# Moving an output eviction forward among a step's convolution taps, and sending a layer norm's variance through PSUM

## The chip, the core and the metric

The kernel runs on one core of a Trainium2 chip. The metric is device time in microseconds. Three runs of the kernel before took 3875.0, 3877.8 and 3879.05 us; the median is 3877.8 us.

## The reference

Two layers are computed on a tensor x of 2 images, 768 channels and 64 × 64 pixels, all in float32. Each is `x = x + layer(group_norm(x))`. The first layer is a Mamba-like block with 1536 inner channels, and the change touches only this one. The second is an attention over tokens with a softmax over heads; it matters here as the work that follows.

```python
x = hs @ in_proj_w.T                                  # 768 -> 1536
xs = depthwise_conv3x3(x) + conv_b                    # 9 taps per channel
xs = xs * sigmoid(xs)
dt, Bs, Cs = split(xs_seq @ x_proj_w.T)
delta = softplus(dt @ dt_w + dt_b)
dA  = exp(delta * A);  dBu = delta * u * Bs           # 4 states per channel
states = scan over tokens: s = dA * s + dBu
y = sum_n(states * Cs) + D_param * u
y = (y - mean(y)) * rsqrt(var(y) + 1e-05) * ln_g + ln_b   # layer norm over the 1536 channels
out = y @ out_proj_w.T                                # 1536 -> 768
```

## The kernel before

The first layer is cut into 16 tiles of 512 tokens (8 image rows), and each tile into 12 chunks of 128 channels. One call of `step(g)` handles one chunk of the scan, and 192 chunks in all (`g` from 0 to 191; tile `g // 12`, chunk `g mod 12`). The same step works on other chunks too: the convolution runs 15 chunks ahead (`a = g + AHEAD`), the input projection 17 ahead (`n`), and the output projection one tile behind (`BEHIND = 12`). The steps run under a manual schedule: each engine executes its instructions in exactly the order in which the Python code issues them, and semaphores hold only what really depends. An engine's queue is strictly in order, so an instruction that waits holds up everything behind it.

What one step issues, engine by engine, as far as it matters here:

- **TensorE (PE):** the input projection (L336), the sums for the layer norm (L518, odd steps), the output projection into the two-bank PSUM tile `po` (L551), in one step of each tile the averages `pm` for the layer norm (L529), and up to one convolution tap as a product with a diagonal matrix (L401), for the next step's chunk.
- **VectorE (DVE):** the convolution taps that are left to it (`taps_dve`, L415: four or five; the first ones accumulate in the PSUM tile `acc`, the last one writes the SBUF tile `u`), then in every fourth step the output's eviction (`out_evict`, L563: two multiplications of `po` by the reciprocal deviation `rs`, into SBUF slots), then the three long instructions of the scan: the input product (L489), the scan itself (L491) and the product with C (L498). In steps with `g mod 12 = 3` it adds the two instructions of the variance (`norm_rs2`, L535 and L536) at the end.
- **ScalarE (ACT):** SiLU (L420, a group of four each fourth step), softplus (L461), the middle tap into `acc` (`tap_act`, L374, which has to wait for the last DVE tap of the chunk before, since `acc` is a single buffer), the input projection's eviction (L349), scaled copies for the taps that a DMA adds (L386), the exponentials of the scan (L466), the output's sums (L585), and the layer norm's square (L531), logarithm (L537) and exponential (L538), the last of which writes `rs`.
- **GpSimd (POOL):** the sum over states (`sum1`, L478), delta times u (`du`, L470, which the input product of the scan in the same step reads), and the issue of accumulating DMAs: convolution taps (L392, L395), the terms of y (L485) and the residual (`out_residual`, L571).
- **SyncE (SP):** plain DMAs: weights, inputs, the store of the result.

`out_evict(g)` evicts what the output projection of the four steps before has accumulated. There is a single `po`, so the first product of the output projection in the same step (L551) waits until both evictions have read it. It happens at `g mod 12` = 4, 8 and 0, three times for each tile. The reciprocal deviation `rs` of a tile is computed at the end of the step with `g mod 12 = 3`; the eviction at `g mod 12 = 4` is the first that uses it. Both `po` evictions have `rs` as their SBUF input and `po` as their PSUM input.

In the steps with an eviction the convolution chunk has `a mod 4 = 3`, and DVE has four taps (3, 5, 7 and 8), three into `acc` and the last into `u`. From `g = 177` on there are no more taps; in those steps the eviction is the first thing that DVE does.

Around the change, in `step`:

```python
if 0 <= a < NQ0:
    taps_dve(a)
if BEHIND < g <= NQ0 + BEHIND and (g - BEHIND) % 4 == 0:
    out_evict(g)
...
if do_c:
    out_proj(g)
if rs_now:
    norm_rs2(g // KI - 1, *norm_rs(g // KI - 1))
if 0 <= a + 1 < NQ0:
    taps_pe(a + 1)
```

Of the kernel before, what the change touches and what calls it, by code (L numbers as in the profile page):

```python
# [9 lines left out]
ALU = mybir.AluOpType  # L10
# [24 lines left out]
NQ0 = NI * KI  # L35
# [17 lines left out]
BEHIND = 12  # L53
# [13 lines left out]
def both_layers(  # L67
# [45 lines left out]
    def take():  # L113
        return slots.pop(0)
# [244 lines left out]
    def dma_taps(a):  # L359
        return DMA_TAPS[a % 4] if a >= AHEAD else ()  # L360

    def pe_taps(a):
        return PE_TAPS[a % 4] if a >= AHEAD else FILL_TAPS
# [39 lines left out]
                skip_group_check=True,  # L403
            )

    def taps_dve(a):
        c = a % KI
        taps = [j for j in range(9) if j != 4 and j not in pe_taps(a) + dma_taps(a)]
        xs, acc = xs_bufs[a % 2], accs.pop(a).rearrange("p (h w) -> p h w", w=W)
        u = take()  # L410
        us[a] = u
        for j in taps:
            dy, dx = divmod(j, 3)
            dst = u.rearrange("p (h w) -> p h w", w=W) if j == taps[-1] else acc
            nc.vector.scalar_tensor_tensor(  # L415
                dst, xs[:, dy : dy + TR, dx : dx + W], pc[:, c, PC_W + j : PC_W + j + 1], acc, ALU.mult, ALU.add
            )

    def silu(a):
        nc.scalar.activation(us[a], us[a], AF.Silu, bias=pc[:, a % KI, PC_CB : PC_CB + 1])  # L420
# [15 lines left out]
    def x_sum(i):  # L436
        px = psX.tile([P, 512], F32, tag="px", name=f"pxs{i}")
        nc.tensor.matmul(px[:XM, :], xsum, pxs["halves"], start=True, stop=True)
        give(pxs.pop("halves"))
        pxs["sum"] = px  # L440
# [91 lines left out]
        return pm, mu2  # L532

    def norm_rs2(i, pm, mu2):
        nc.vector.scalar_tensor_tensor(mu2, mu2, -1.0, pm[:, 1, :], ALU.mult, ALU.add)  # L535
        nc.vector.tensor_scalar_max(mu2, mu2, 0.0)  # L536
        nc.scalar.activation(rs, mu2, AF.Ln, bias=eps_c)  # L537
        nc.scalar.activation(rs, rs, AF.Exp, scale=-0.5)  # L538

# [17 lines left out]
    def out_evict(g):  # L557

        po = pos[0]
        i, r = (g - 1 - BEHIND) // KI, (g - 1) % KI  # L560
        for e in range(2):
            xr = take()
            nc.vector.tensor_mul(xr, po[:, e, :], rs)  # L563
            xrs[i, 2 * (r // 4) + e] = xr
# [311 lines left out]
    with tc.manual_schedule():  # L876
# [17 lines left out]
        def step(g, prep=None):  # L894
            a, n = g + AHEAD, g + AHEAD + 2
# [27 lines left out]
                norms[g][0][1]()  # L923
            if xd_now:
                x_sum(g // KI + 1)
            if 0 <= a < NQ0:
                taps_dve(a)
            if BEHIND < g <= NQ0 + BEHIND and (g - BEHIND) % 4 == 0:
                out_evict(g)
            for q in range((v - 1) * PER_STEP, min(v * PER_STEP, N_PIECE)):  # L930
                if q >= 0:
                    gn_piece(1, q)
# [96 lines left out]
            if rs_now:  # L1029
                norm_rs2(g // KI - 1, *norm_rs(g // KI - 1))  # L1030
# [16 lines left out]
        with tc.tile_pool(name="l0st", bufs=1, side="right") as sp:  # L1047
            wg = out_weights_load(sp)
            for g in range(-AHEAD - 2, -1):
                step(g, (lambda: out_weights(sp, wg)) if g == -AHEAD + 5 else None)  # L1050
                if g >= -AHEAD + 7:
                    for k in ((g + AHEAD - 7) * 2, (g + AHEAD - 7) * 2 + 1):
                        if k < KI:
                            out_weights_store(wg, k)
# [10 lines left out]
        for g in range(-1, NQ0 + 2):  # L1065
            step(g)
# [18 lines left out]
        for g in range(NQ0 + 2, NQ0 + BEHIND + 3):  # L1085
            step(g)
# [12 lines left out]
@with_exitstack  # L1099
def mamba_then_attention(  # L1100
    ctx, tc, x, in_wP, xp_wP, dt_wP, out_wT, pc_in, comb_in, pick_in, xsum_in, qkvP, woutP, temp_c, ident_in, gavg_in, gsel_in, hcol_in, hsel_in, esel_in, out
):
    nc = tc.nc
    keep = ctx.enter_context(tc.tile_pool(name="keep", bufs=1))
    dram = ctx.enter_context(tc.tile_pool(name="dram", bufs=1, space=DRAM))
    x1 = [dram.tile([DM, L], F32, name=f"x1_{b}") for b in range(NB)]

    stats1 = [keep.tile([P, KM, 2 * NT + 1], F32, name=f"stats1_{b}") for b in range(NB)]

    ident = keep.tile([P, P], F32, name="ident")  # L1110
    nc.sync.dma_start(ident, ident_in)
    ones = keep.tile([P, P], F32, name="ones")
    nc.vector.memset(ones, 1.0)
    eps_c = keep.tile([P, 1], F32, name="eps_c")
    nc.vector.memset(eps_c, EPS)
    consts = (ident, ones, eps_c)


    wo_dr = dram.tile([KM // 2, KI // 3, P, 3, 2 * P], F32, name="wo_dr")
    bc_dr = [dram.tile([2 * NS, TL], F32, name=f"bc_dr{i}") for i in range(NI)]  # L1120
    both_layers(
        tc, nc, consts, x, in_wP, xp_wP, dt_wP, out_wT, pc_in, comb_in, pick_in, xsum_in, gavg_in, gsel_in, wo_dr, bc_dr, x1, stats1,
        qkvP, woutP, temp_c, hcol_in, hsel_in, esel_in, [out[b].rearrange("c h w -> c (h w)") for b in range(NB)],
    )
# [104 lines left out]
```

## Time and profile before

| what | value |
|---|---|
| median of three runs | 3877.8 us |
| the profiled execution's own time | 3880.97 us |
| its span | 3879.2 us |
| mean granted TensorE clock | 0.985 |
| busy PE / DVE / ACT / POOL | 3643.6 / 2792.9 / 2459.8 / 1657.2 us |
| evictions L563: count, median | 96, 682 ns |
| variance L535 and clamp L536: count, median | 16 each, 680 ns and 1731 ns |
| taps L415 into `acc`: count, mean | 753, 754 ns |
| taps L415 into `u`: count, mean | 192, 748 ns |

The span is that of one execution under the profiler; the device time lies 1.8 us above it. A row of the profile's groups names the line, the engine, the operation, the output and inputs by the program's names, and the shapes; then busy time and mean duration; then the idle time of the engine just ahead of these instructions, and what ended it. The first layer's steps with scans and taps fill the span from about 380 to 2580 us; the scans without taps end near 2800 us, and the attention layer fills the rest.

### The profile page before, as it was taken

How to read it: one execution, taken by the hardware profiler on the slowest of the kernel's cores; microseconds unless marked ns; L12 is line 12 of the kernel's file. 1: busy time of each engine (PE TensorE's matmuls, PEld its weight loads, DVE VectorE, ACT ScalarE, POOL GpSimd, SP SyncE). 2: the span in 40 equal slices, each digit the busy share in tenths (PEclk: the TensorE clock that was granted, in tenths of full speed). 3: DMA queues.
4: the chain of work that ended last, by engine and by line, in shares of the span. 5: the costliest groups of instructions: out<-in, count | busy, mean ns of one | idle time of the engine just before them, and what ended most of it. 6: DMA issues, size and time to landing. Idle time of an engine off the chain costs nothing.

```text
span 3879.2 us, 32882 instructions
## 1 busy us (share of the span) xinstructions
PE 3643.6 (94%) x9798; PEld 1512.8 (39%) x9798; DVE 2792.9 (72%) x2339; ACT 2459.8 (63%) x4667; POOL 1657.2 (43%) x1494
## 2 busy tenths in 40 slices
PE   4977999999999999999999999999999999998999
PEld 2422333333333333333433333333344444444444
DVE  5699999999999999999999999987400520005311
ACT  1378888888898888888888888886423511123000
POOL 0435556555655655655555655554300011111222
PEclk9988999999999999999999999999999999999999
DMA  7466898888888889889888898886543245442454
GB/s 278 160 177 134 187 205 180 201 202 194 203 182 200 205 188 207 179 202 213 172 203 183 202 206 184 198 176 168 146 126 129 68 145 154 150 140 83 142 179 154
DMA packets 321574, 679.65 MB, mean 175 GB/s; under 512 B 37378, under 2 KB 45572, under 8 KB 317300
## 3 DMA queue, kind: packets, MB, share of 16 engines
q0 software_dynamic: 139248, 253.56, 38.2%
q1 hardware_dynamic: 182148, 424.00, 33.4%
q8 instruction: 78, 1.28, 0.1%
q14 instruction: 100, 0.82, 0.1%
HBM read 393.77 MB, written 55.31 MB: 116 GB/s over the span
## 4 chain that ended last, share of the span: by engine, by line
DVE 45%; PE 34%; ACT 7%; issue 6%; DMA 5%; POOL 3%; SPq 0%; DVEq 0%; POOLq 0%; ACTq 0%
DVE s L491 17%; PE mm L665 13%; DVE acc L415 9%; PE mm L638 9%; DVE da L498 8%; DVE s L489 7%; PE pa L336 3%; PE po L551 3%; DMA tm<-tm 2%; PE pq L638 2%; DMA u<-tm 2%; POOL ysum L478 1%; DMA u<-ysum 1%; DVE u L563 1%; ACT da L466 1%
## 5 line engine op out<-in xcount | busy, mean ns | idle before, releaser
L551 PE MATMUL po<-u,w 128*128 128x512 f32 x2304 | 1047.8, 605 | 69.1 <-DVE u L563 68.7
L336 PE MATMUL pa<-u,w 128*128 128x512 f32 (+1 forms) x2304 | 1040.0, 601 | 0.0
L491 DVE TENSOR_TENSOR_SCAN s<-da,s 128x2052 f32<-128x2052 f32 x192 | 851.1, 4433 | 19.2 <-DVE s L489 0.5
L551 PEld LDWEIGHTS po<-u,w 128*128 128x128 f32 x2304 | 431.5, 192 | 673.8 <-issue 569.1
L336 PEld LDWEIGHTS pa<-u,w 128*128 128x128 f32 x2304 | 430.4, 192 | 591.4 <-issue 529.0
L478 POOL TENSOR_TENSOR ysum<-da 128x1024 f32<-128x1024 f32 x192 | 396.7, 2066 | 533.1 <-DVE da L498 506.9
L415 DVE SCALAR_TENSOR_TENSOR acc<-xs,pc,acc 128x512 f32<-128x512 f32 x753 | 567.8, 754 | 70.3 <-PE acc L401 50.3
L466 ACT ACTIVATE da<-dl,neg_a 128x512 f32<-128x512 f32 x768 | 489.6, 713 | 0.0
L660 POOL TENSOR_TENSOR w<-w,at 128x768 f32<-128x768 f32 x96 | 141.0, 1470 | 814.9 <-DMA w<-woutP 562.5
L392 POOL DMA_DIRECT2D tm<-tm x310 | 273.9, 885 | 500.5 <-ACT tm L386 444.9
L489 DVE TENSOR_TENSOR s<-du,bc 128x2048 f32<-128x2048 f32 x192 | 438.8, 2285 | 66.0 <-POOL du L470 63.8
L498 DVE TENSOR_TENSOR da<-s,bc 128x2048 f32<-128x2048 f32 x192 | 440.0, 2292 | 6.3
L485 POOL DMA_DIRECT2D u<-ysum x384 | 391.7, 1314 | 0.5 <-POOL ysum L478 0.3
L665 PE MATMUL mm<-u,w 128*128 128x512 f32 x684 | 320.8, 596 | 0.0
L386 ACT ACTIVATE tm<-xs,pc 128x512 f32<-128x512 f32 x487 | 317.7, 718 | 2.8 <-DMA tm<-tm 2.8
L674 DVE TENSOR_TENSOR u<-mm,u 128x512 f32<-128x512 f32 x59 | 40.8, 692 | 337.8 <-PE mm L665 337.8
L374 ACT ACTIVATE acc<-xs,pc 128x512 f32<-128x512 f32 x192 | 132.6, 690 | 211.7 <-DVE u L415 210.8
L470 POOL TENSOR_TENSOR du<-dl,u 128x512 f32<-128x512 f32 x192 | 258.7, 1348 | 0.0
L395 POOL DMA_DIRECT2D u<-tm x177 | 218.7, 1235 | 83.5 <-DMA tm<-tm 64.5
L665 PE MATMUL mm<-v,w 128*128 128x512 f32 x468 | 225.7, 593 | 0.0
L638 PE MATMUL mm<-u,w 128*128 128x512 f32 x456 | 214.4, 594 | 0.0
L665 PEld LDWEIGHTS mm<-u,w 128*128 128x128 f32 x684 | 129.3, 191 | 167.6 <-issue 167.4
(206 smaller groups left out, 4060.1 us busy)
## 6 DMA issues: line engine op xcount, KB each, us to landing
u<-ysum POOLq DMA_DIRECT2D x384, 256.0 KB, 5.8
tm<-tm POOLq DMA_DIRECT2D x310, 256.0 KB, 4.7
w<-in_wP SPq DMA_DIRECT2D x192, 384.0 KB, 4.3
w<-wo_dr SPq DMA_DIRECT2D x192, 384.0 KB, 5.1
u<-x SPq DMA_DIRECT2D x254, 256.0 KB, 4.3
u<-tm POOLq DMA_DIRECT2D x177, 256.0 KB, 5.8
w<-qkvP SPq DMA_DIRECT2D x96, 384.0 KB, 3.1
w<-woutP SPq DMA_DIRECT2D x96, 384.0 KB, 3.7
```

The lines of the kernel that those rows point to most:

```text
L336: nc.tensor.matmul(pa[:, :nn], w[:, k, :], xts[i, k][:, :nn], start=(k == 0), stop=(k == KM - 1))
L386: nc.scalar.activation(tm.rearrange("p (h w) -> p h w", w=W), xs[:, dy : dy + TR, dx : dx + W], AF.Copy, scale=pc[:, c, PC_W + j : PC_W + ...
L415: nc.vector.scalar_tensor_tensor(dst, xs[:, dy : dy + TR, dx : dx + W], pc[:, c, PC_W + j : PC_W + j + 1], acc, ALU.mult, ALU.add)
L466: nc.scalar.activation(das[g % 2][:, n, 1:], deltas[g], AF.Exp, scale=neg_a[:, c, n : n + 1])
L478: nc.gpsimd.tensor_add(ysum[:, 0 : 2 + g % 2 : 1 + g % 2, :], da[:, 0:2, 1:], da[:, 2:4, 1:])
L485: nc.gpsimd.dma_start(us[g], ysums(g, n), accum_op=ALU.add)
L489: nc.vector.tensor_mul(s[:, :, 1:], dus.pop(g).unsqueeze(1).to_broadcast([P, NS, TL]), bc[:, :NS, :])
L491: nc.vector.tensor_tensor_scan(sf, das[g % 2].rearrange("p n l -> p (n l)"), sf, 0.0, ALU.mult, ALU.add)
L498: nc.vector.tensor_mul(das[g % 2][:, :, 1:], s[:, :, 1:], bc[:, NS:, :])
L551: nc.tensor.matmul(po[:, e, :], w[:, kk, e * P : (e + 1) * P], us[i * KI + k], start=(k == 0), stop=(k == KI - 1))
L638: nc.tensor.matmul(pa, w[:, k, :], x1s[b, j, k], start=(k == 0), stop=(k == KM - 1))
L665: nc.tensor.matmul(po, w[:, k, :], w1s[b, k, j], start=(k == 0), stop=(k == KM - 1))
```

## The change

There are two edits. `taps_dve` takes a function and calls it after it has issued the first tap; `step` passes it the eviction in the steps that have one. So on DVE the two evictions stand behind the first tap and ahead of the other three. In steps without taps the eviction is issued where it was. `norm_rs2` writes the difference of mean square and squared mean to the first half of the PSUM tile `pm`, whose contents have been read by then, and the clamp at zero reads it there and writes the SBUF tile `mu2` as before.

```diff
-    def taps_dve(a):
+    def taps_dve(a, after_first):
...
             nc.vector.scalar_tensor_tensor(
                 dst, xs[:, dy : dy + TR, dx : dx + W], pc[:, c, PC_W + j : PC_W + j + 1], acc, ALU.mult, ALU.add
             )
+            if j == taps[0]:
+                after_first()
...
     def norm_rs2(i, pm, mu2):
-        nc.vector.scalar_tensor_tensor(mu2, mu2, -1.0, pm[:, 1, :], ALU.mult, ALU.add)
-        nc.vector.tensor_scalar_max(mu2, mu2, 0.0)
+        nc.vector.scalar_tensor_tensor(pm[:, 0, :], mu2, -1.0, pm[:, 1, :], ALU.mult, ALU.add)
+        nc.vector.tensor_scalar_max(mu2, pm[:, 0, :], 0.0)
...
+            evict = (lambda: out_evict(g)) if BEHIND < g <= NQ0 + BEHIND and (g - BEHIND) % 4 == 0 else (lambda: None)
             if 0 <= a < NQ0:
-                taps_dve(a)
-            if BEHIND < g <= NQ0 + BEHIND and (g - BEHIND) % 4 == 0:
-                out_evict(g)
+                taps_dve(a, evict)
+            else:
+                evict()
```

## Prediction

> **What bounds the kernel now.** I read the page first: engine shares, chain that ended last, costliest groups.
>
> ```profile
> PE 3643.6 (94%) x9798; PEld 1512.8 (39%) x9798; DVE 2792.9 (72%) x2339; ACT 2459.8 (63%) x4667; POOL 1657.2 (43%) x1494
> DVE 45%; PE 34%; ACT 7%; issue 6%; DMA 5%; POOL 3%; SPq 0%; DVEq 0%; POOLq 0%; ACTq 0%
> L551 PE MATMUL po<-u,w 128*128 128x512 f32 x2304 | 1047.8, 605 | 69.1 <-DVE u L563 68.7
> ```
>
> By shares PE looks like the bound, and its one large idle entry is 68.7 us ahead of the out projection, waiting for the eviction that the change moves. But the chain runs more through DVE. So I split by stage: first a window (its length, then busy us of PE, PEld, DVE, ACT and POOL, each with a count, granted clock, DMA share, GB/s), then the waits of DVE and of PE inside 440 to 2500 us, where the scan steps run together with the conv taps (us in total, times, longest).
>
> ```profile
> 1000.00:1300.00 300.00, 286.70 (x750) 113.50 (x749) 290.24 (x189) 260.11 (x513) 174.22 (x162) 1.00 0.89 198
> ```
>
> ```profile
> DVE s L489 <- POOL du L470: 12.0, 13, 2.3
> DVE mu L535 <- ACT mu L531: 3.6, 3, 3.2
> DVE s L489 <- ACT u L585: 1.8, 4, 0.5
> ```
>
> ```profile
> PE po L551 <- DVE u L563: 54.8, 34, 3.5
> ```
>
> In those 2060 us DVE waits 12.0 + 3.6 + 1.8 + 0.5 (a last row, not shown) = 18 us in all, and never for PE; PE waits 55 us for DVE. **DVE sets the pace and PE follows.** The scans' starts (L491) say it step by step: 12.89 us for most steps, 13.29 with an eviction, 15.58 with an eviction and the layer norm's variance. What PE gets back is worth nothing unless it shortens DVE's queue. So I take DVE's timeline at one variance (start, us, engine, line):
>
> ```profile
> 595.10 0.68 DVE L535 SCALAR_TENSOR_TENSOR mu<-mu,pm 128x512 f32<-128x512 f32 x1
> 595.82 1.73 DVE L536 TENSOR_SCALAR mu<-mu 128x512 f32<-128x512 f32 x1
> 597.47 2.33 DVE L415 SCALAR_TENSOR_TENSOR acc<-xs,pc,acc 128x512 f32<-128x512 f32 x3
> 599.83 0.75 DVE L415 SCALAR_TENSOR_TENSOR u<-xs,pc,acc 128x512 f32<-128x512 f32 x1
> 600.50 1.28 DVE L563 TENSOR_TENSOR u<-po,rs 128x512 f32<-128x512 f32 x2
> 601.69 2.28 DVE L489 TENSOR_TENSOR s<-du,bc 128x2048 f32<-128x2048 f32 x1
> ```
>
> and ACT's and POOL's beside it:
>
> ```profile
> 597.58 0.72 ACT L537 ACTIVATE rs<-mu,eps_c 128x512 f32<-128x512 f32 x1 [2.53 <-DVE mu L536]
> 598.34 0.63 ACT L538 ACTIVATE rs<-rs 128x512 f32<-128x512 f32 x1
> ```
>
> ```profile
> 595.27 2.00 POOL L478 TENSOR_TENSOR ysum<-da 128x1024 f32<-128x1024 f32 x1 [3.45 <-DVE da L498]
> ```
>
> The clamp (L536) takes 1.73 us here, ending just after POOL's addition does (597.27). Its own line gives 426/1731/1786 ns as min/median/max.
>
> [...] 1.73 us beside POOL's addition, 0.43 us at 2821.8 us, where POOL is idle. [...] No wide clamp from PSUM is in the trace. [...] the trace shows an independent successor starting about 0.08 us before an end, a dependent one 0.03 to 0.04 after it.
>
> **The variance.** L535 keeps its operands and writes PSUM in place of SBUF; conv taps take 754 ns to PSUM and 748 to SBUF, so nothing is charged (bounds 0 to 0.1 us each). The clamp now reads PSUM. Nearest row: L563, one PSUM input, 682 ns. Bounds: 0.43 (still fast) to 1.73 (still blocked). I take 0.68.
>
> **The eviction.** Two L563 and no DMA (its residual DMA stays) move past three taps in DVE's queue alone, in the 41 eviction steps that have taps. PE's, ACT's, POOL's and SP's orders stay. A tap that reads the tap before it costs 0.79 from start to start (2.36/3), an independent follower 0.67, an eviction 0.60. Before: 3 × 0.787 + 0.67 + 1.19 = 4.22. After: 0.67 + 1.19 + 2 × 0.787 + 0.67 = 4.10, as the evictions fill one dependence gap: **0.12 us less**. PE's po is ready, as the first tap already waits for PE work that stands behind it.
>
> In 14 steps (g mod 12 = 4) the eviction is the first to read the new rs and comes before ACT has it. From the clamp's end to an eviction that waits for rs is 1.45 us (2823.70 − 2822.25; the same at 2677.8). With the clamp's start as zero: first tap 0.60, rs at 0.68 + 1.45 = 2.13, evictions to 3.32, two taps to 4.89, the last to 5.57, then L489. Before, L489 came at (clamp − 0.08) + 4.22. The gain is thus clamp − 1.43: of the 1.05 us saved on a blocked clamp, about 0.85 comes back as a wait for rs that three taps used to hide, with three taps queued behind it. The 14 clamps read 0.64, 1.73, 1.46, 1.73, 1.46, 1.55, 1.73, 1.73, 1.73, 0.45 and four of 1.73: 21.13 us. Gain 21.13 − 20.02 = **1.1 us**.
>
> In 14 steps (g mod 12 = 8) rs is old: 14 × 0.12 = **1.7 us**. In 13 steps (g mod 12 = 0) the next L489 waits for a chain outside DVE:
>
> ```profile
> 545.75 7.75 DMA tm<-tm
> 554.05 6.34 DMA u<-tm
> ```
>
> POOL stands 4.5 us behind the first transfer before it can compute du. 0.12 is lost again in 12 of these, kept in one: **0.1 us**. After the taps the eviction doesn't move; of the two clamps there, the blocked one (1.79 us) has both DVE and PE behind it, **1.1 us**, and the other (0.43 to 0.68) ends inside a PE product, 0.
>
> Against it: the last tap ends 1.2 us later beside the scan, and behind it on ACT are L374 and all of that step. ACT's waits of 2 to 5 us for the tap cover that, and later a 3 us wait for a tap's DMA (g mod 12 = 1) or 1.1 us and more of POOL idle plus 0.42 us of slack (g mod 12 = 6). One step (scan at 1964.6, 15.06 us long) shows no such cover: −**1.2 us**.
>
> Sum: 1.1 + 1.7 + 0.1 + 1.1 − 1.2 = 2.8 us. The profiled execution (3880.97 us, span 3879.2) would become 3878.2; it lies 3.2 above the median of the runs, 3877.8, which becomes **3875.0**. Own range 3871 to 3879, chance 0.52. A measurement of this kernel can tell about 0.2% (7.8 us) from no change; this is within it.
>
> **Rivals.**
> *PE's stall was worth its size* (0.14). For it: PE is 94% busy. Against it: DVE never waits for PE in the window. All of 54.8 us gives 3823; half, 3850.
>
> *The DMA chain moves* (0.16). PE ends its products up to 2 us sooner, so weight loads start sooner, beside the tm transfer above (7.75 us where its median is 4.7). A shift of 0.6 us in 13 places is 8 us either way: 3867 to 3883.
>
> *ACT falls late* (0.12, slower). If the 1.2 us are not covered, POOL's L392, L395, addition and du move with ACT, and L489 waits. One place in 14 tiles is 17 us: 3892. It decides once the shift passes 1.1 + 0.42 = 1.5 us; the cover in the profile speaks against it.
>
> *The clamp stays blocked* (0.06, slower). With a mean of 1.51 us from PSUM as before, 14 × 0.83 plus 1.1 are lost: 3875.0 + 12.7 = 3888. The gain is gone at about 0.87 us a clamp; slower by 0.2% is reached near 1.4.
>
> **The numbers.** Faster: 0.04 of the forecast, 0.13 of the stall, 0.06 of the DMA chain = 0.23. Slower: 0.01, 0.05 of the DMA chain, 0.10 of ACT, 0.05 of the clamp = 0.21. Within 0.2%: 0.56. The range of 3862 to 3890 holds the forecast, the DMA chain and the blocked clamp; it leaves out most of the stall case and the worst of ACT's.
>
> **What would show it.** Right: clamps near 0.68 us everywhere; PE's wait for L563 nearly gone in 440 to 2500 us; a new DVE wait of L563 on ACT's rs, some 0.85 us in 14 steps; those steps at 15.3 us in place of 15.58, those with g mod 12 = 8 at 13.17 in place of 13.29. Wrong: steps without an eviction shorter than 12.89 (PE had paced them), more than 12 us of L489 waiting for du (ACT late), or clamps still over 1 us.

## The result, and the profile after

The changed kernel takes 3889.86 us (median of 14 runs, 3883.29 to 3897.15) where the kernel before takes 3879.8 us (median of 14, 3875.0 to 3884.3): a ratio of 1.0028, 95% interval 1.002 to 1.0036. It is about 10 us slower, where 2.8 us of gain were forecast.

From line 417 on, the changed kernel's line numbers are two higher than before: the out projection is L553, the eviction L565, variance and clamp L537 and L538, the input product L491, the scan L493, `du` L472, `sum1` L480.

The page of the changed kernel: engine shares, the chain that ended last, and the costliest group.

```profile
PE 3661.4 (94%) x9798; PEld 1513.1 (39%) x9798; DVE 2776.7 (71%) x2339; ACT 2453.6 (63%) x4667; POOL 1651.4 (42%) x1494
PE 41%; DVE 39%; DMA 7%; ACT 6%; issue 5%; POOL 2%; SPq 0%; DVEq 0%; POOLq 0%; ACTq 0%
L553 PE MATMUL po<-u,w 128*128 128x512 f32 x2304 | 1037.8, 600 | 25.2 <-DVE u L565 25.2
```

DVE has become 16 us less busy and PE's idle time ahead of the out projection has fallen from 69.1 to 25.2 us, as meant. But PE is busy 17.8 us longer with the same 9798 instructions, and the chain runs less through DVE and more through PE and DMA. The longer busy time is the first trace of what went wrong: the same products took longer. The trace's record of the clock granted to TensorE accounts for about as much. From the scan of `g = 10` to that of `g = 175` the clock stood at 0.50 for 34.1 us before and for 71.7 us after; the 37.6 us more at half rate are 18.8 us of work.

The waits of the changed kernel in 440 to 2500 us (us in total, times, longest):

```profile
PE acc L401 <- ACT acc L374: 52.6, 20, 6.5
...
POOL ysum L480 <- DMA u<-ysum: 31.3, 15, 5.9
DVE s L491 <- POOL du L472: 25.4, 17, 3.1
...
PE po L553 <- DVE u L565: 15.9, 24, 2.4
...
DVE u L565 <- ACT rs L540: 10.3, 13, 0.8
...
DVE pm L537 <- ACT mu L533: 8.4, 9, 1.5
```

and the line of the clamp (count, then min/median/max in ns):

```profile
L538 DVE TENSOR_SCALAR mu<-pm x16: 690/691/692, 437.9 to 2829.5; 128x512 f32<-128x512 f32 x16
```

What the change does directly is what was forecast: every clamp takes 0.69 us, PE's wait for the eviction is down from 54.8 to 15.9 us, and the eviction waits for `rs` in 13 places, 10.3 us. What was not forecast are the others. DVE waits for `du` 25.4 us (12.0 before) and for ACT's square 8.4 us (3.6 before); POOL's `sum1` waits 31.3 us for the DMAs of y (1.6 before); and PE waits 52.6 us for ACT ahead of its tap L401 (17.4 before).

Sums of the times from one scan's start to the next (DVE's timeline), by the step that ends at the scan, in one profiled execution of each kernel; 14 steps each, 13 for the last row. All other columns of `g mod 12` agree within 0.1 us.

| g mod 12 | before | after | change | forecast |
|---|---|---|---|---|
| 0 | 185.27 | 186.34 | +1.07 | −0.1 |
| 1 | 197.27 | 205.88 | +8.61 | 0 |
| 2 | 184.74 | 181.62 | −3.12 | 0 |
| 4 | 220.19 | 225.53 | +5.34 | −1.1 |
| 8 | 172.80 | 171.07 | −1.73 | −1.7 |

These make up the +10.15 us of the stretch from the scan of `g = 10` to that of `g = 175`. So there are two places to explain: steps with `g mod 12 = 1`, which hold no eviction and no variance at all, and steps with 4.

**Steps with g mod 12 = 1.** The same tile in both kernels, with the scan of `g = 47` as zero: it starts at 853.68 before and at 855.22 after. SP's queue, before and then after (start, us, queue, line):

```profile
863.81 0.33 SPq L303 DMA_DIRECT2D w<-in_wP  x1
870.17 0.32 SPq L309 DMA_DIRECT2D w<-wo_dr  x1
870.54 0.49 SPq L287 DMA_DIRECT2D u<-x  x1
```

```profile
863.46 0.33 SPq L303 DMA_DIRECT2D w<-in_wP  x1
869.34 0.32 SPq L309 DMA_DIRECT2D w<-wo_dr  x1
869.71 0.83 SPq L287 DMA_DIRECT2D u<-x  x1
```

Less the zero, the three loads start at 10.13, 16.49 and 16.86 us before, and at 8.24, 14.12 and 14.49 after: about 2 us sooner. They wait for buffers that PE's products release, and PE no longer stalls at the eviction. POOL's DMAs of y start at 10.60 in both (864.28 and 865.82). They take longer to land, before and then after:

```profile
DMA to landing us min/median/max: 8.9/9.3/9.7
```

```profile
DMA to landing us min/median/max: 9.3/10.0/10.8
```

Then POOL and DVE in the changed kernel:

```profile
877.33 2.00 POOL L480 TENSOR_TENSOR ysum<-da 128x1024 f32<-128x1024 f32 x1 [1.06 <-DMA u<-ysum]
879.30 1.26 POOL L472 TENSOR_TENSOR du<-dl,u 128x512 f32<-128x512 f32 x1
880.59 2.29 DVE L491 TENSOR_TENSOR s<-du,bc 128x2048 f32<-128x2048 f32 x1 [1.63 <-POOL du L472]
```

`sum1` waits 1.06 us for the landing, `du` stands behind it in POOL's queue and starts as it ends, and the input product waits 1.63 us for `du` (0.44 us at this place before). At this place the bound is the chain through DMA and POOL and not DVE: the small wait that the profile of before shows here was the sign of a chain with nothing to spare. Whether the earlier loads are what lengthens the landing is left to the experiments.

**Steps with g mod 12 = 4.** PE's tap L401 three steps earlier, at the end of the step with `g mod 12 = 1` in the same tile, before and then after:

```profile
884.14 1.13 PE L401 MATMUL acc<-xs,dg 128*128 128x512 f32 x2 [1.25 <-ACT acc L374]
```

```profile
885.51 2.07 PE L401 MATMUL acc<-xs,dg 128*128 128x512 f32 x2 [3.45 <-ACT acc L374]
887.52 3.68 PE L429 MATMUL px<-u,xp_w 128*64 128x512 f32 x8
```

PE is early, so it waits longer for ACT, in one piece of 3.45 us, and behind that piece its instructions take almost twice as long: 2.07 us for 1.13, and 3.68 us for the 1.94 that the same products (L427) took before. The windows over the same stretch show the clock, in the column ahead of the last two: before in one row, after in two.

```profile
884.00:889.00 5.00, 4.86 (x15) 1.76 (x16) 4.89 (x5) 5.00 (x11) 2.52 (x3) 1.00 0.75 200
```

```profile
882.00:885.40 3.40, 0.06 (x1) 0.00 (x0) 3.30 (x2) 3.36 (x6) 1.15 (x2) 0.91 1.07 203
885.40:891.00 5.60, 5.49 (x10) 1.27 (x10) 5.53 (x4) 5.60 (x12) 2.69 (x3) 0.50 0.92 207
```

In the trace's record the clock stands at 0.50 from 884.80 to 891.62 us. It is no single case: in the changed kernel 12 of the 14 tiles have such a stretch at this place (one in the kernel before), the starts lie whole multiples of 3.413 us apart, and the stretches last one, two or three times 3.41 us. In the 3.41 us ahead of these stretches PE was busy for 0.24 to 1.36 us, and in one tile the idle piece ahead of L401 was 2.93 us long. In another an idle piece of 3.43 us was not followed by the half rate; it lay across a point of this grid, with 1.45 us of work in the one cell of 3.41 us and 1.95 in the next. The two traces show no sharp bound: in the attention layer of the kernel before a cell with 1.95 us of work (3605.48 to 3608.89 us) was followed by a clock of 0.50. What sets the clock is not shown; that the idle piece ahead of L401 has a part in it is shown by e4_filler.

Having lost its lead, PE is late with the next input projection, ACT waits for it, and DVE's variance waits for ACT. The two waits are 20 us apart; that the one leads to the other is shown by e4_filler and not by these lines:

```profile
896.82 0.58 ACT L349 COPY xs<-pa 128x512 f32<-128x512 f32 x1 [1.58 <-PE pa L336]
```

```profile
917.07 0.70 DVE L537 SCALAR_TENSOR_TENSOR pm<-mu,pm 128x512 f32<-128x512 f32 x1 [1.55 <-ACT mu L533]
917.79 0.69 DVE L538 TENSOR_SCALAR mu<-pm 128x512 f32<-128x512 f32 x1
918.40 0.74 DVE L415 SCALAR_TENSOR_TENSOR acc<-xs,pc,acc 128x512 f32<-128x512 f32 x1
919.94 1.29 DVE L565 TENSOR_TENSOR u<-po,rs 128x512 f32<-128x512 f32 x2 [0.79 <-ACT rs L540]
```

The clamp, the one tap and the wait of 0.79 us for `rs` are as forecast; the 1.55 us ahead of the variance (none before at this place) come on top. Over the 14 tiles: in seven the clock stood at 0.50 for 6.8 us or more, and their steps with 4 took 16.24 to 16.94 us; in five for 3.4 us, and these took 15.31 to 15.60 in four and 16.77 in the fifth (17.59 in the same tile before); the two tiles without took 15.58 and 15.30.

A late variance also costs more than it did. In the kernel before the clamp ended 9.12 us after the scan in 13 of the 14 tiles, 0.28 us behind POOL's addition, whether it took 0.64 or 1.73 us: a variance that waited up to 1.01 us for ACT's square left the step at 15.59. The clamp that reads PSUM took 0.69 us in all 16 places, 15 of them beside an instruction of POOL, and so each late variance lengthens the step by what it waits, as here: 1.55 us of wait, and a step of 16.94 us in place of 15.31.

### The profile page after: what moved, and what is told of

The parts are those of the page before. It is cut to its first block, busy times and chain, and to the rows that moved or that the text cites. A ratio compares the mean times of both kernels' runs of the same rounds, so it can differ in the third digit from the quotient of the medians.

```text
span 3888.0 us, 32882 instructions
## 1 busy us (share of the span) xinstructions
PE 3661.4 (94%) x9798; PEld 1513.1 (39%) x9798; DVE 2776.7 (71%) x2339; ACT 2453.6 (63%) x4667; POOL 1651.4 (42%) x1494
## 4 chain that ended last, share of the span: by engine, by line
PE 41%; DVE 39%; DMA 7%; ACT 6%; issue 5%; POOL 2%; SPq 0%; DVEq 0%; POOLq 0%; ACTq 0%
DVE s L493 15%; PE mm L667 13%; PE mm L640 9%; DVE acc L415 8%; DVE da L500 7%; DVE s L491 6%; PE pa L336 5%; PE po L553 5%; DMA tm<-tm 2%; PE pq L640 2%; DMA u<-tm 2%; DMA u<-ysum 1%; PE px L429 1%; POOL ysum L480 1%; PE acc L401 1%
## 5 line engine op out<-in xcount | busy, mean ns | idle before, releaser
L553 PE MATMUL po<-u,w 128*128 128x512 f32 x2304 | 1037.8, 600 | 25.2 <-DVE u L565 25.2
L493 DVE TENSOR_TENSOR_SCAN s<-da,s 128x2052 f32<-128x2052 f32 x192 | 851.1, 4433 | 19.2 <-DVE s L491 0.5
L553 PEld LDWEIGHTS po<-u,w 128*128 128x128 f32 x2304 | 429.0, 191 | 620.6 <-issue 568.3
L415 DVE SCALAR_TENSOR_TENSOR acc<-xs,pc,acc 128x512 f32<-128x512 f32 x753 | 567.5, 754 | 69.1 <-PE acc L401 50.6
L480 POOL TENSOR_TENSOR ysum<-da 128x1024 f32<-128x1024 f32 x192 | 386.9, 2015 | 527.0 <-DVE da L500 460.2
L491 DVE TENSOR_TENSOR s<-du,bc 128x2048 f32<-128x2048 f32 x192 | 438.9, 2286 | 78.4 <-POOL du L472 77.9
L487 POOL DMA_DIRECT2D u<-ysum x384 | 380.7, 1259 | 1.1 <-issue 0.8
L472 POOL TENSOR_TENSOR du<-dl,u 128x512 f32<-128x512 f32 x192 | 246.8, 1285 | 0.0
L401 PE MATMUL acc<-xs,dg 128*128 128x512 f32 x208 | 121.9, 670 | 85.4 <-ACT acc L374 84.6
```

The source lines that it names most:

```text
L415: nc.vector.scalar_tensor_tensor(dst, xs[:, dy : dy + TR, dx : dx + W], pc[:, c, PC_W + j : PC_W + j + 1], acc, ALU.mult, ALU.add)
L480: nc.gpsimd.tensor_add(ysum[:, 0 : 2 + g % 2 : 1 + g % 2, :], da[:, 0:2, 1:], da[:, 2:4, 1:])
L487: nc.gpsimd.dma_start(us[g], ysums(g, n), accum_op=ALU.add)
L491: nc.vector.tensor_mul(s[:, :, 1:], dus.pop(g).unsqueeze(1).to_broadcast([P, NS, TL]), bc[:, :NS, :])
L493: nc.vector.tensor_tensor_scan(sf, das[g % 2].rearrange("p n l -> p (n l)"), sf, 0.0, ALU.mult, ALU.add)
L553: nc.tensor.matmul(po[:, e, :], w[:, kk, e * P : (e + 1) * P], us[i * KI + k], start=(k == 0), stop=(k == KI - 1))
```

## The experiments

The theories were: **loads** (PE's lead starts SP's loads early, and they slow the DMAs of y), **clock** (PE's waiting in one piece is followed by a granted clock of 0.50), and against them **ACT** (the last tap is 1.2 us later in the eviction steps, and with it everything behind it on ACT).

In the expectations theory P stands for loads and clock together and theory A for ACT. Each run is compared with the kernel before as measured in its own series, so differences between runs are best taken from the ratios. In the kernels with stores (e5 to e10) most line numbers are two higher again.

Step sums of the profiled executions, as in the table above, and the ratio to the kernel before with its 95% interval:

| kernel | g mod 12 = 1 | 2 | 4 | ratio |
|---|---|---|---|---|
| before | 197.27 | 184.74 | 220.19 | |
| after | 205.88 | 181.62 | 225.53 | 1.0028 (1.002 to 1.0036) |
| e1_variance | 198.07 | 185.26 | 208.94 | 0.9965 (0.9953 to 0.9978) |
| e2_evict | 208.26 | 182.47 | 232.99 | 1.0052 (1.0039 to 1.0064) |
| e3_third | 202.68 | 182.69 | 206.35 | 0.9965 (0.9953 to 0.9978) |
| e4_filler | 209.42 | 182.07 | 217.04 | 1.0007 (0.9999 to 1.0015) |
| e5_hold | 191.67 | 269.29 | 224.56 | 1.0232 (1.0212 to 1.0252) |
| e6_third_hold | 193.01 | 279.76 | 212.82 | 1.0201 (1.0187 to 1.0215) |
| e7_hold_filler | 194.33 | 283.19 | 224.00 | 1.0232 (1.0218 to 1.0246) |
| e8_hold_one | 197.67 | 186.92 | 229.12 | 1.0016 (1.0008 to 1.0024) |
| e9_third_one | 195.58 | 183.71 | 206.40 | 0.9964 (0.9952 to 0.9977) |
| e10_both | 196.26 | 186.41 | 214.93 | 0.9988 (0.998 to 0.9996) |

### e1_variance: the variance edit alone

```diff
-        nc.vector.scalar_tensor_tensor(mu2, mu2, -1.0, pm[:, 1, :], ALU.mult, ALU.add)
-        nc.vector.tensor_scalar_max(mu2, mu2, 0.0)
+        nc.vector.scalar_tensor_tensor(pm[:, 0, :], mu2, -1.0, pm[:, 1, :], ALU.mult, ALU.add)
+        nc.vector.tensor_scalar_max(mu2, pm[:, 0, :], 0.0)
```

Against the kernel before; the eviction stays behind the last tap.

> The variance's edit alone; the eviction stays behind all taps. Theory P (TensorE ahead): the loss of the whole change comes from the early eviction alone, so here 21.1 us of clamps in the 14 steps with taps become 14 x 0.69 = 9.7 us, three taps still hide the wait for rs, and 1.1 us more is won after the taps: about 12.5 us faster than before (ratio near 0.9968), with the variance steps at about 14.5 us in place of 15.58. Rival V (the way through PSUM costs what it saves): no gain, or slower than before.

Measured: 3868.49 us beside 3881.59 us, 13.1 us less. The steps with `g mod 12 = 4` give 11.25 us of it, those with 1 stay where they were. This edit alone is a gain, and the forecast's prices of the clamp hold.

### e2_evict: the eviction alone

```diff
             if 0 <= a < NQ0:
-                taps_dve(a)
-            if BEHIND < g <= NQ0 + BEHIND and (g - BEHIND) % 4 == 0:
-                out_evict(g)
+                taps_dve(a, evict)
+            else:
+                evict()
```

> The early eviction alone; the variance stays in SBUF. If the two edits simply add, this is the whole change less the first experiment's gain: 10 + 12.5 = some 22 us slower than before (ratio near 1.006), variance steps at 16.3 us and more because the wait for rs now stands behind a blocked clamp, steps with g mod 12 = 1 at 14.8 us. If the late clamp hides part of what is late in the whole change (theory P: TensorE's products for the mean), less: 12 to 18 us slower.

Measured: 3902.27 us, 20.7 us more than before. Both slow columns are there (208.26 and 232.99), and e1_variance has neither, so the losses start with the eviction's place. Column 4 is not the clock's alone here. The wait for `rs` now stands behind a clamp that is still blocked (0.43 to 1.78 us, median 1.17), as was expected at 16.3 us a step, and ten of the 14 steps took 16.33 to 16.34 us although the variance waited up to 0.8 us for ACT's square in them; only four took longer. So what a late square costs in the full change (11 us over its 14 steps, against 15.31 each) depends on both edits. The times nearly add up: −13.1 + 20.7 = 7.6, and together they made 10.1.

### e3_third: the full change, the eviction behind the third tap

```diff
-            if j == taps[0]:
+            if j == taps[-2]:
                 after_first()
```

> The whole change with the eviction behind the third tap of four, one place before where it was. The last tap still ends 1.2 us later than before, but TensorE gets po only 0.8 us sooner in place of 2.4. Theory P (TensorE ahead, so weight loads meet the DMAs of y, and its idle time gathers in one piece): steps with g mod 12 = 1 back near 13.7 us, no half-rate products, rs never waited for; 12.5 us of the variance and 27 x 0.12 = 3 us of the gap: 14 to 16 us faster than before. Theory A (ScalarE late because the last tap ends later): the steps with g mod 12 = 1 stay at 14.7 us, and the gain is some 5 to 8 us only.

Measured: 3869.47 us, 12.1 us less than before. PE's lead is smaller, and so is the loss in the steps with 1; it is not gone as expected. With 14.48 us median it lies nearer to theory A's 14.7 than to P's 13.7, so this run doesn't decide between them. The loads still start 0.7 to 0.8 us early, at 9.47, 15.70 and 16.07 us in the tile shown. The clock's loss is gone where it counted (14.65 us median with `g mod 12 = 4`), though PE still has short slow pieces, here 1.94 us for the 1.13 of before:

```profile
881.13 1.94 PE L401 MATMUL acc<-xs,dg 128*128 128x512 f32 x2 [2.78 <-ACT acc L374]
```

### e4_filler: the full change, with work for PE in its idle piece

Three products that add zero to `po` stand at the end of the out projection in the steps with `g mod 12 = 1`.

```diff
+        if r == 1 and g < NQ0 - AHEAD:
+            for _ in range(3):
+                nc.tensor.matmul(po[:64, 0, :], zeros[:, :64], us[i * KI + k], start=False, stop=False)
```

> The whole change, and in steps with g mod 12 = 1 three products by a block of zeros more behind the output projection (some 2.7 us of TensorE time where it idles 3.4 us; they add zero to po). Theory P: TensorE keeps its full rate, the products behind the idle time take 1.0 and 1.9 us again in place of 2.1 and 3.7, the mean for the variance is in time, and the variance steps fall from a mean of 16.1 to 15.3 us: about 5 to 6 us faster than the whole change, 4 to 5 slower than before. Steps with g mod 12 = 1 stay at 14.8. Theory A: no change against the whole change, 10 us slower than before.

Measured: 3884.45 us (13 runs), 5.4 us less than the changed kernel (8 by the ratios, each to the kernel before in its own series). PE's timeline in the same tile:

```profile
881.31 2.79 PE L560 MATMUL po<-u,zeros 128*64 128x512 f32 x6
884.34 1.13 PE L401 MATMUL acc<-xs,dg 128*128 128x512 f32 x2 [0.24 <-ACT acc L374]
885.40 1.94 PE L429 MATMUL px<-u,xp_w 128*64 128x512 f32 x8
```

With 2.79 us of empty work in the gap, L401 and what follows run at their old durations, here and in ten other tiles; in three the clock still falls to 0.50 for 3.4 us. The steps with `g mod 12 = 4` fall to 15.31 us median, the forecast's 15.3, and DVE's wait for ACT's square from 8.4 to 2.0 us. The steps with 1 stay slow (209.42), as the clock theory says nothing of them. PE works more and the kernel is faster, with intervals of the ratios that lie apart: this shows the clock's part.

### e5_hold, e6_third_hold, e7_hold_filler: the loads held back, badly

Two small stores on SP's queue, each of one column of 128 rows, read a tile that is written late, so that the loads behind them start later; alone, with the third tap, and with the filler.

```diff
+            if g % KI == 1 and BEHIND < g < NQ0 - AHEAD:
+                nc.sync.dma_start(hold_dr[1], us[g - 1][:, :1])
...
+            if g % KI == 0 and BEHIND < g < NQ0 - AHEAD:
+                nc.sync.dma_start(hold_dr[0], us[a][:, :1])
```

> The whole change, with SyncE held back twice in a tile (after the step with g mod 12 = 0): a 512-byte store that waits for the last tap stands ahead of the next input weights, and one that waits for ScalarE's product of D and u ahead of the next output weights. The loads that moved from 10.1 to 8.2 us and from 16.5 to 14.1 us after the scan's start go back to about 10.9 and 15.6. Theory P (loads meet the DMAs of y): those DMAs land within some 9.5 us again in place of 11, and the steps with g mod 12 = 1 fall from 14.8 to about 13.8 us (those with g mod 12 = 2 rise from 12.9 to 13.2): about 8 us faster than the whole change, near or just above before. Theory A (the later last tap moves the ScalarE and GpSimd work behind it): the loads don't matter, 14.8 stays, no change against the whole change.

> The eviction behind the third tap with the variance through PSUM, and the same two holds. Theory P: steps with g mod 12 = 1 fall from 14.5 to about 13.7 us, 5 to 7 us faster than without the holds: some 19 us faster than before (ratio near 0.995). Theory A: 14.5 stays, ratio 0.9965 as without.

> The whole change with the two holds and with the three zero products on TensorE in the steps with g mod 12 = 1. If the loss has these two causes and no third, both of its parts go: variance steps at 15.3 us, steps with g mod 12 = 1 at 13.8: the forecast's 2.8 us faster than before, give or take 3. If a third cause remains, it stays slower than before by 2 us or more.

Measured: 3969.68, 3961.12 and 3971.08 us, 80 to 91 us slower than before. The instrument was wrong. The waits of e5_hold, first of SP's queue, then of the engines:

```profile
SPq L1054 <- DMA u<-tm: 165.1, 12, 14.7
```

```profile
ACT u L424 <- DMA hold<-u: 97.9, 12, 9.2
POOL u L489 <- DMA hold<-u: 92.0, 12, 9.2
...
DVE acc L417 <- PE acc L403: 48.3, 12, 5.1
```

The first store stands in the program behind the DMAs that add taps to the same chunk, and waits for them, so SP's whole queue is held 13.8 us on average; and ACT, whose SiLU writes that chunk next, waits 8.2 us for the store. The second reads a tile into which POOL next adds a term of y, and POOL waits 7.7 us for it. The steps with 2 take 19.79 us median, for 12.89 in the changed kernel. The larger part of that comes through the first store: ACT is late with `acc`, PE waits for it ahead of its tap L403, and DVE waits for PE, 4.0 us on average in 12 places, where in this stretch it didn't wait for PE at all before. But one thing can be read: in the step ahead of it, with `g mod 12 = 1`, no load starts while its DMAs of y run (the last ones start 7.7 us after the scan, these DMAs 10.6 us). They land within 7.9 us median, and the step takes 12.91 us median, that is, no wait at all. Its accumulating DMA on POOL still comes as late as in the changed kernel, in e5_hold at

```profile
885.50 0.85 POOL L394 DMA_DIRECT2D tm<-tm  x1 [1.39 <-ACT tm L388]
```

which is 14.05 us after the scan at 871.45, where it was 14.05 in the changed kernel (869.27 − 855.22) and 12.99 before (866.67 − 853.68). ACT is late by the same 1.06 us and nothing comes of it: the ACT theory falls for these steps.

### e8_hold_one: the loads held back by one element

The stores now copy one element; the first is issued right behind the DVE taps and waits for the last tap alone, the second stands ahead of the weight load.

```diff
+            if g % KI == 1 and BEHIND < g < NQ0 - AHEAD:
+                nc.sync.dma_start(hold_dr[1], us[g - 1][:1, :1])
             if BEHIND <= g + 1 < NQ0 + BEHIND:
                 load_wo(g + 1)
...
                 taps_dve(a, evict)
+                if g % KI == 0 and BEHIND < g < NQ0 - AHEAD:
+                    nc.sync.dma_start(hold_dr[0], us[a][:1, :1])
```

> The whole change, with SyncE held back by two stores of one element in place of 128: the first stands right behind the last tap in program order, ahead of the DMA that adds to the same tile, so it waits for the last tap and for nothing later; the second waits for ScalarE's product of D and u. Input weights then start near 10.9 us after the scan in place of 8.2, output weights near 15.6 in place of 14.1, and the stores end long before GpSimd's DMAs write the same tiles. Theory P: the steps with g mod 12 = 1 fall from 14.8 us to 13.6 to 13.9, those with g mod 12 = 2 rise to 13.2 at most: 5 to 8 us faster than the whole change. Theory A: 14.8 stays.

SP's queue in the same tile, with the zero at 859.24:

```profile
870.12 0.24 SPq L936 DMA_DIRECT2D hold<-u  x1
870.46 0.33 SPq L305 DMA_DIRECT2D w<-in_wP  x1
874.77 0.24 SPq L908 DMA_DIRECT2D hold<-u  x1
875.10 0.55 SPq L311 DMA_DIRECT2D w<-wo_dr  x1
875.69 0.76 SPq L289 DMA_DIRECT2D u<-x  x1
```

The loads start at 11.22, 15.86 and 16.45 us, close to the kernel before. The median landing of the DMAs of y over the tiles goes from 10.15 us in the changed kernel to 9.4 (9.1 before), and the steps with 1 go from 205.88 to 197.67, the 197.27 of the kernel before. That shows the loads' part in these steps. The time, though, is 3886.87 us (15 runs), only 3 us less than the changed kernel (5 by the ratios, whose intervals overlap) where 5 to 8 were expected, and its profiled execution shows no gain (scans of `g = 10` to 175: 2212.51 us for 2212.03). The next step, with 2, gives back 5.3 us, presumably since the loads that are moved out of the one lie beside the other (not tried apart), and the steps with 4 lose 3.6 us more than in the changed kernel (229.12), with the half rate in all 14 tiles (at 570.23 and 730.73 us the products L431 take 3.43 and 3.68 us for 1.94).

### e9_third_one: third tap and one-element stores

The edits of e3_third and e8_hold_one.

> The eviction behind the third tap, the variance through PSUM, and the same two stores of one element. Theory P: steps with g mod 12 = 1 fall from 14.5 to about 13.8 us: 4 to 8 us faster than without the stores, some 17 to 21 us faster than before (ratio 0.9945 to 0.9955). Theory A: ratio 0.9965 as without.

Measured: 3864.63 us, 15.2 us less than before, the lowest median of all; the ratio, 0.9964, was expected at 0.9945 to 0.9955. The steps with 1 gain 7.1 us against e3_third and those with 2 lose 1.0 in the profiled executions, but by the intervals it can't be told from e3_third, or from e1_variance.

### e10_both: one-element stores and filler

The edits of e4_filler and e8_hold_one on the full change: both causes taken away, the eviction still behind the first tap.

> The whole change with the one-element holds and with the three zero products. If the loss has these two causes alone, variance steps fall to 15.3 us and those with g mod 12 = 1 to 13.8: the forecast's 2.8 us faster than before, give or take 3. If a third cause remains, it stays slower than before by 2 us or more.

Measured: 3875.67 us (13 runs), 4.2 us less than before (ratio 0.9988, 0.998 to 0.9996, that is 1.6 to 7.8 us less). The waits of e10_both:

```profile
PE acc L403 <- ACT acc L376: 23.3, 28, 1.7
```

```profile
DVE pm L539 <- ACT mu L535: 0.2, 1, 0.2
```

No idle piece of PE ahead of L403 is longer than 1.7 us, the clock stands at 1.00 throughout from 383 to 2673 us (the products L431 take 1.94 us in all 42 places), and DVE's wait ahead of the variance is gone. Each part shows in the time as well. Against e8_hold_one the filler takes the ratio from 1.0016 to 0.9988; against e4_filler the stores take it from 1.0007 (0.9999 to 1.0015) to 0.9988 (0.998 to 0.9996), with intervals that just lie apart.

The forecast's gain of 2.8 us lies in the interval, so no third cause is needed, though one of about 1 us could hide in it. That the sum fits is in part luck. The steps with 4 gain 5.3 us where 1.1 was forecast, since late variances that the kernel before had, and the forecast kept, are gone too (one tile's step took 17.59 us before and takes 15.48), and the steps with 1 and 2 together lose 0.7 us.

## Why the prediction was wrong

- **The clamp** was right: 0.68 us forecast, the author's estimate from L563 (682 ns), and 0.69 measured in all 16. Why the source in PSUM makes the difference is not shown.
- **The rs wait** was right: 0.85 us in 14 steps forecast; 10.3 us in 13 places measured, 0.79 each. Without the clock's loss (e10_both) these steps took 15.31 us median; 15.3 was forecast.
- **The dependence gap** was right: 1.7 us forecast with `g mod 12 = 8`, 1.73 measured (13.16 us a step for a forecast of 13.17).
- **The tail** was right in size: 1.1 us forecast, 0.98 measured (scans of `g = 175` to 191: 204.65 to 203.67).
- **ACT falls late**: 1.2 us were charged in one step and the rival was given 0.12. The lateness is there (1.06 us), but where it could be watched alone, in the steps with `g mod 12 = 1` of e5_hold, it cost nothing. The mark set for it, over 12 us of the input product waiting for `du`, was reached (25.4 us), and would have convicted the wrong cause: the same wait has another releaser, the landing of the DMAs of y.
- **The other two rivals** are ruled out: no clamp was blocked, and PE's stall was not worth its size, as 39 us less of it made the kernel slower.
- **The step that failed** is "What PE gets back is worth nothing unless it shortens DVE's queue". It was used as a bound on the gain and, without being said, as a bound on the loss. PE's lead was priced at nothing. It had a price, and two places of it were missed. First, loads that PE releases start 2 us sooner and collide with the DMAs of y: +8.6 us in the steps with 1, −3.1 in those behind them. Second, PE's waiting moved from the evictions (54.8 to 15.9 us) to one piece ahead of L401 (17.4 to 52.6 us), and the half rate behind it makes ACT's square late, which the unblocked clamp no longer hides: where a gain of 1.1 us was forecast for `g mod 12 = 4`, 5.34 were lost, 6.4 in all. e4_filler takes 8.5 off these steps, somewhat more, as DVE waited for ACT's square in the kernel before too (3.6 us in 3 places, 2.0 with the filler). The half rate itself is not new. Before, five tiles had it for 3.4 us at the stall ahead of the out projection (L551), and their steps with 4 still took 15.58 or 15.59 us: there it lay where nothing in DVE's queue waited for PE.
- **The rival "The DMA chain moves"** had the right cause, loads released sooner by PE, but the wrong victim (the taps' transfers `tm`; it was the DMAs of y) and the wrong place, 13 steps with an eviction (they changed by 1.07 us, which was not followed up). Its size, 8 us either way, was about that of the loss in the steps with 1, by luck, as it was reckoned for another place.

The forecast named a stall that goes and asked only who would be glad of it. The question "what is late next" was answered for DVE and ACT, and not for the engine that was freed.

## What to carry to other kernels

A stall that is taken from an engine with slack moves on: look for where that engine waits next, and how long in one piece, and what stands behind that piece, since here the same waiting cost nothing ahead of one product and 6 us ahead of another. An engine that runs ahead also frees its buffers sooner, and the loads behind them start sooner, here by 2 us and beside transfers with no time to spare; list what it releases before pricing its lead at nothing. Of two edits made together, try each alone: here one was worth −13 us and the other +21.

## What was not expected of the hardware

- In a stage in which TensorE is busy for 1989 of 2060 us (440 to 2500 us of the changed kernel), its granted clock fell to 0.50 after single idle pieces, and a pair of products took 2.07 us for 1.13. The falls lie whole multiples of 3.413 us apart, and in the 3.41 us ahead of them PE had been busy for up to 1.36 us in the changed kernel's 12 tiles and up to 1.39 in the five of the kernel before. The shortest idle pieces that were followed by one are 2.93 us ahead of L401 in the changed kernel and 2.09 us ahead of L551 in the kernel before, where four of nine pieces of 2.09 to 2.13 us were.
- Loads from SP's queue that start 2 us sooner made POOL's accumulating DMAs of y land about 1 us later (median 9.1 to 10.15 us).
- A store of one column of 128 rows held the next writer of its tile: in e5_hold ACT's SiLU waited 97.9 us in 12 places for it, 8.2 each, and POOL's DMA 92.0 us in 12, 7.7 each (6.85 in the tile shown, up to 902.79 us). In e8_hold_one, with a single element and the first store moved forward, nobody waited for either; which of the two differences did it was not tried apart.
- From SBUF to SBUF the clamp took 0.64 to 1.79 us in the 14 places where an instruction of POOL ran beside it and 0.43 and 0.45 us in the two where none did, and in 13 of the 14 tiles of the kernel before it ended 0.28 us behind POOL's addition; from PSUM it took 0.69 us in all 16 places, 15 of them beside an instruction of POOL.
